# Cross-attention on one core: product 7 of y split once more in batches 3 to 6 and 8, T4 formed by ScalarE and accumulating DMAs in batches 3 to 8

## The chip, the core and the metric

The kernel runs on one core of one Trainium2 chip. Its engines work side by side, each through its own instructions in order: TensorE (PE, with its weight loads shown apart as PEld) multiplies matrices into PSUM, VectorE (DVE) and ScalarE (ACT) work element by element and read PSUM, GpSimd (POOL) reduces over partitions and issues DMAs, SyncE (SP) issues DMAs. Every wait between engines is a semaphore. The metric is the time of one execution in microseconds of the device; all times below are microseconds unless ns stands beside them.

## The reference

Eight batches; x (called x1 in the kernel) and ctx (x2) are 8 x 512 x 1024, FP32.

```python
q = jnp.einsum('bcn,dc->bnd', x1, Wq) + bq
k = jnp.einsum('bcn,dc->bdn', x2, Wk) + bk[:, None]
v = jnp.einsum('bcn,dc->bdn', x2, Wv) + bv[:, None]
attn = jax.nn.softmax(jnp.einsum('bnd,bdm->bnm', q, k), axis=2)
attn_out = jnp.einsum('bcm,bnm->bcn', v, attn)
return attn_out + x1
```

D is 64, C is 512, N is 1024. Since each row of attn sums to one, the kernel multiplies in another order: y = x2 times the transposed attn, then out = Wv y + bv + x1.

## The kernel before

Numbers of batches: the code counts `s.b` from 0 to 7, so batch 3 of the title is `s.b == 2`, and batch 8 is `s.b == 7`.

**Two stages, seven products each.** Stage y (`first(i)` in `period`) multiplies the 512 x 1024 matrix x2 by the 1024 x 1024 matrix of exponentials, stage o (`second(i)`) multiplies Wv by y. Both use Winograd's form of Strassen's scheme: each operand is cut into 2 x 2 blocks, four sums are made of the left blocks (S1 to S4) and four of the right ones (T1 to T4), and seven products take the place of eight. `MULT` (L290) lists for each product its two operands and its PSUM bank: products 1, 6, 5 and 3 add up in bank a, 7 and 4 in bank c (2 opens bank c and leaves block 11 there). Each bank is a pair of tiles, a0 and a1 or c0 and c1, for the two halves j of 128 rows. After products 1, 6 and 5, ScalarE copies the running sum out of bank a into `s.tmp[i]` (tags u1, u6, u5; L323), since the result blocks need each of the partial sums. `RESULT` (L456) says what each block is: 11 = bank c + u1, 22 = bank c after product 7 + u5, 12 = bank a after product 3, 21 = bank c after product 4 + u6. VectorE forms these in `evict_y` and `evict_o`; in stage y, step 1 adds, step 2 multiplies by the reciprocal denominators `rden`.

**A second cut.** Some products of stage y are themselves computed by the same scheme, with blocks of 128 x 256: `multiply_2`, `multiply_3` and `multiply_4`. `inner_left` and `inner_right` make the eight inner sums on VectorE (L344, L355), `inner_product` (L358) multiplies. In `multiply_onto` (used for 3 and 4) the inner products 2, 4 and 3 go straight onto the outer bank (`b0` left, `b1` left, `b0` right); inner product 1, then 6, then 5 add up in a buffer `chain` of the two-buffer tag `sc`, and 7 goes to `third`, the other `sc` buffer. ScalarE copies chain after 1, after 6 and twice after 5 into `d`, and third into `v` (L371); then `complete` adds v to d on VectorE (L431), and what d holds is added to the result. The inner products run in the order 1, 7, 6, 2, 5, 4, 3.

**Softmax.** The scores of the next batch n, two halves h of four tiles i, are multiplied in between (L190), by way of `sc` buffers and, for i = 2, bank c (h = 0) or bank a (h = 1). ScalarE copies them out (`e`, L199 and L197), VectorE folds the maximum over tiles (L210, L214), GpSimd reduces it over partitions (`highest`, L220), VectorE subtracts it (`lower`, L248) and ScalarE exponentiates (L252). Denominators: for h = 0 `start_sum` copies tile 0 on ScalarE and adds the others by accumulating DMAs of POOL (`add_tile`, L521); for h = 1 VectorE adds (L210). `total` reduces over partitions on POOL (L225) and starts a DMA (`few`); `shares` takes the reciprocal (L233) and spreads it by DMAs of POOL.

**Order.** The whole order is written by hand (`manual_schedule`): each engine runs what it is given in the order in which `period` (L671) calls it. In batches 2 to 5 (as `s.b` counts) it reads: first(1); T1, T2 and the sums of h = 1; multiply_2 and its evictions; T4 (`sum_t4`, L270), S4 and T3 on VectorE; first(6); the inner sums of T4 and S4; the scores of h = 0 and the next queries; their maxima; first(5); `lower` and the exponentials; inner sums of product 3's right operand; first(7); inner sums of block 22; multiply_3; blocks 22 and 12 out of PSUM; multiplication by `rden`; the scores of h = 1 and the next keys; T1, T2 of y; multiply_4; block 21; then second(1), 6, 2, 5, 7, 3, 4 with their evictions, and between them the sums and inner sums of the next batch. Batch 7 has no next batch: no scores, queries or keys stand between its products.

**Buffers.** Tags with one buffer tie steps together: eT4 holds T4 and, at the end of a period, the inner sums for the next batch's product 2; eT2 holds T2 and then the inner sums of T4; u5 holds product 5's copy and then product 4's d; i2 is multiply_2's; yT1, yT2, yT4 and y12 hold sums and blocks of y in stage o. x2 and x1 of later batches are loaded through one buffer x (L125), block tiles of x2's transpose by L132, results go out by L517 (x1 added to them by an accumulating DMA of POOL) and L518.

Of the kernel before, what the change touches and what calls it, by code (L numbers as in the profile page):

```python
# [15 lines left out]
def kernel(  # L16
# [8 lines left out]
    bv: bass.AP,  # L25
    out: bass.AP,
):

# [71 lines left out]
    def left_sums(a, *ks):  # L100

        for k in ks:
            x, y, op = {
                "S1": ("21", "22", ALU.add),
                "S2": ("S1", "11", ALU.subtract),
                "S3": ("11", "21", ALU.subtract),
                "S4": ("12", "S2", ALU.subtract),
            }[k]
            nc.vector.tensor_tensor(a["21" if k == "S3" else k], a[x], a[y], op)  # L109
            if k == "S3":  # L110
                a["S3"] = a["21"]
# [145 lines left out]

    def right_sums(t, k):

        x, y = {"T1": ("12", "11"), "T2": ("22", "T1"), "T3": ("22", "12"), "T4": ("21", "T2")}[k]  # L260
        nc.vector.tensor_tensor(t[k], t[x], t[y], ALU.subtract)  # L261

    def open_t(s):
        for n in ("T1", "T2"):
# [3 lines left out]
        s.t["T3"] = s.t["12"]  # L268

    def sum_t4(s):  # L270
        s.t["T4"] = sb.tile([P, MH, H], F32, tag="eT4", name=f"eT4_{s.b}")
        sum_e(s, "T4")

    def sum_e(s, *ks):
        for i in (0, 2):
            part = {n: v[:, i : i + 2, :] for n, v in s.t.items()}
            for k in ks:
                right_sums(part, k)
# [18 lines left out]
        4: ("22", "T4", "c", False),  # L297
    }

    def multiply(s, stage, i, left, right, n_k, last=False):  # L300


        ka, kb, bank, opens = MULT[i]
        for j in range(2):
            if opens:
                s.bank[bank, j] = ps_a.tile(
                    [P, H], F32, tag=f"{bank}{j}", name=f"ps_{stage}{bank}{j}_{s.b}_{i}"
                )
            ps = s.bank[bank, j]
            for n in HALVES if last and j else (slice(0, H),):  # L310
                for k in range(n_k):
                    nc.tensor.matmul(  # L312
                        ps[:, n],
                        left[ka][:, k, ts(j, P)],
                        right[kb][:, k, n],
                        start=opens and k == 0,
                        stop=i in (2, 3, 4) and k == n_k - 1,
                        skip_group_check=True,
                    )
            if i in (1, 6, 5):  # L320
                if j == 0:
                    s.tmp[i] = sb.tile([P, 2, H], F32, tag=f"u{i}", name=f"u{stage}{i}_{s.b}")
                nc.scalar.copy(s.tmp[i][:, j, :], ps)  # L323

    LEFT = (
        ("S1", "21", "22", ALU.add),
        ("S2", "S1", "11", ALU.subtract),
        ("S3", "11", "21", ALU.subtract),
        ("S4", "12", "S2", ALU.subtract),
    )  # L330
    RIGHT = (
        ("T1", "12", "11", ALU.subtract),
        ("T2", "22", "T1", ALU.subtract),
        ("T3", "22", "12", ALU.subtract),
        ("T4", "21", "T2", ALU.subtract),
    )
# [10 lines left out]
    def inner_right(s, i, x, tag):  # L347
# [4 lines left out]
        sums = sb.tile([P, 4, MH // 2, H // 2], F32, tag=tag, name=f"eI{i}_{s.b}")  # L352
        for z, (k, x, y, op) in enumerate(RIGHT):
            v[k] = sums[:, z]
            nc.vector.tensor_tensor(v[k], v[x], v[y], op)  # L355
        s.inner[i, "t"] = v

    def inner_product(s, i, z, ps, opens, *copies):  # L358

        ka, kb, _, _ = MULT[z]  # L360
        for k in range(MH // 2):
            nc.tensor.matmul(  # L362
                ps,
                s.inner[i][ka][:, k, :],
                s.inner[i, "t"][kb][:, k, :],
                start=opens and k == 0,
                stop=z in (2, 3, 4) and k == MH // 2 - 1,
                skip_group_check=True,
            )
        for copy in copies:  # L370
            nc.scalar.copy(copy, ps)  # L371
# [35 lines left out]

        return evict

    def multiply_onto(s, i, d_tag, v_tag):  # L410

        b0, b1 = (s.bank[MULT[i][2], j] for j in range(2))
        chain, third = inner_bank(s, i, 0), inner_bank(s, i, 2)
        d = sb.tile([P, 2, 2, H // 2], F32, tag=d_tag, name=f"d{i}_{s.b}")
        v = sb.tile([P, 2, H], F32, tag=v_tag, name=f"v{i}_{s.b}")[:, 0, left]
        for z, ps, opens, *copies in (
            (1, chain, True, d[:, 0, 0, :]),
            (7, third, True, v),  # L420
            (6, chain, False, d[:, 1, 0, :]),
            (2, b0[:, left], False),
            (5, chain, False, d[:, 0, 1, :], d[:, 1, 1, :]),
            (4, b1[:, left], False),
            (3, b0[:, right], False),
        ):
            inner_product(s, i, z, ps, opens, *copies)

        def complete():
            both = v.unsqueeze(1).to_broadcast([P, 2, H // 2])  # L430
            nc.vector.tensor_tensor(d[:, 1], d[:, 1], both, ALU.add)  # L431

        return d.rearrange("p j a n -> p j (a n)"), complete

    def multiply_4(s):

        d, complete = multiply_onto(s, 4, "u5", "r")
        complete()
        for j in range(2):
            u6 = s.tmp[6][:, j, :]  # L440
            nc.vector.tensor_tensor(u6, u6, d[:, j, :], ALU.add)

    def multiply_3(s):

        d, complete = multiply_onto(s, 3, "u1", "r")

        def evict():
            complete()
            s.y["12"] = y = sb.tile([P, 2, H], F32, tag="y12", name=f"y12_{s.b}")
            for j in (1, 0):  # L450
                nc.vector.tensor_tensor(y[:, j, :], s.bank["a", j], d[:, j, :], ALU.add)

        return evict
# [4 lines left out]
    def evict_y(s, k, steps=(1, 2)):  # L458

        bank, add = RESULT[k]  # L460
        rden = s.rden.get(int(k[1]) - 1)
        if 1 in steps:
            s.y[k] = sb.tile([P, 2, H], F32, tag=f"y{k}", name=f"y{k}_{s.b}")
        y = s.y[k]
        for step in steps:
            for j in range(2):
                ps = s.bank.get((bank, j))
                if add is None and step == 1:
                    nc.vector.tensor_tensor(y[:, j, :], ps, rden, ALU.mult)
                elif step == 1:  # L470
                    nc.vector.tensor_tensor(y[:, j, :], ps, s.tmp[add][:, j, :], ALU.add)
                else:
                    nc.vector.tensor_tensor(y[:, j, :], y[:, j, :], rden, ALU.mult)

# [45 lines left out]
    def add_tile(s, h, i):  # L520
        nc.gpsimd.dma_start(s.mx[h], s.e[h][:, :, i, :], accum_op=ALU.add)  # L521

    def start_sum(s, h):

        e = s.e[h]
        s.mx[h] = f = sb.tile([P, 2, H], F32, tag="fold", name=f"sum_{s.b}_{h}", bufs=2)
        nc.scalar.copy(f, e[:, :, 0, :])
        for i in range(1, MH if s.b > 1 else 2):  # L530
            add_tile(s, h, i)

# [138 lines left out]
    def period(s, n, nn, nnn):  # L671

        def first(i):
            multiply(s, "y", i, s.a, s.t, MH)

        def second(i):
            multiply(s, "o", i, w, s.y, 2, n is None and i == 3)
# [31 lines left out]
        if n:  # L711
            load_a(n, "21", "22")
        first(6)
        if s.b:
            inner_right(s, 4, s.t["T4"], "eT2")
            inner_left(s, 3, s.a["S4"], "aI3")

        def next_queries():
            queries(nn)
# [17 lines left out]
        first(5)  # L737
        if s.b == 0:
            inner_right(s, 3, s.t["22"], "eT1")
            for i in range(MH):  # L740
                lower(n, 0, i)
        elif n:
            for i in range(MH):
                exponentials(n, 0, i)
            start_sum(n, 0)
        if s.b:
            inner_right(s, 3, s.t["22"], "eT1")
        first(7)
        if s.b > 1:
            inner_left(s, 4, s.a["22"], "a12")  # L750
        evict_3 = multiply_3(s)
        if s.b:
            evict_y(s, "22", (1,))
            evict_3()
        else:
            evict_3()
            evict_y(s, "22", (1,))
        for k in ("11", "12", "22"):
            evict_y(s, k, (2,))
        if s.b == 1:  # L760
# [102 lines left out]
```

## Time and profile before

Three runs took 695.27, 695.43 and 696.22; the median is 695.43. One execution was profiled:

| | |
|---|---|
| profiled execution, its time | 694.83 |
| its span, first to last instruction | 693.0 |
| granted TensorE clock | 1.00 throughout |
| VectorE, sum of T2 or T4, 128x1024 (L261 eT<-e,eT) | 32 of them, mean 1489 ns |
| VectorE, inner sums of a right operand, 128x512 (L355) | 683 to 688 ns each |
| VectorE, inner sums of a left operand, 128x256 (L344) | 418 to 497 ns each |
| ScalarE, copy of 128x512 out of PSUM (L323) | 587 ns |
| ScalarE, copy of 128x1024 in SBUF (L529) | 1031 ns |
| ScalarE, copy of an inner product, 128x256 (L371) | 372 to 375 ns |
| POOL, issue of an accumulating DMA (L521) | 1224 ns, landing 5.1 later (median) |
| POOL, all-reduce of a denominator (L225) | mean 4337 ns |
| POOL, all-reduce of a maximum (L220) | mean 1957 ns |

The mean of one instruction is from its start to its end; VectorE and ScalarE overlap the end of one with the start of the next by some 0.1, so that a sequence is read from start to start in the timeline. First(1) of the batches starts at 204.0 (`s.b` = 2), 288.4, 372.7, 457.2, 541.7 and 619.5 (`s.b` = 7).

### The profile page before, as it was taken

The numbers are of one execution on the slowest core, as the hardware profiler recorded it, in microseconds if no ns is written. First come the engines' busy times: TensorE is split into PE (matmuls) and PEld (weight loads), VectorE is DVE, ScalarE is ACT, GpSimd is POOL, SyncE is SP. The second block draws the span as 40 slices with busy tenths as digits, with TensorE's granted clock in tenths as the row PEclk, the third lists the DMA queues.
The fourth block names the chain that finished last, engine by engine and source line by source line (L and its number), as shares of the span: only waits on it lengthen the run. The fifth ranks groups of instructions, "written<-read, shape, count | busy, mean of one in ns | idle before, by whom it ended". The sixth has DMA issues, their size and how long they took to land.

```text
span 693.0 us, 6395 instructions
## 1 busy us (share of the span) xinstructions
PE 685.8 (99%) x2188; PEld 353.4 (51%) x2188; DVE 604.5 (87%) x756; ACT 255.2 (37%) x402; POOL 186.9 (27%) x135
## 2 busy tenths in 40 slices
PE   8999999999999999999999999999999999999997
PEld 5333554535545355454654546454554545545563
DVE  1999999988999878998789987999689998999685
ACT  2733353145242543235432344413444235241120
POOL 0123113512322125222162222522223222423000
PEclk9999999999999999999999999999999999999999
DMA  9676256953567463865639457284742743369103
GB/s 307 254 233 226 58 183 129 260 157 76 183 128 210 149 116 142 166 183 151 107 138 191 157 166 181 67 190 140 183 78 55 172 136 60 77 115 251 31 1 121
DMA packets 42992, 102.72 MB, mean 148 GB/s; under 512 B 4688, under 2 KB 6992, under 8 KB 42960
## 3 DMA queue, kind: packets, MB, share of 16 engines
q1 hardware_dynamic: 25856, 70.13, 29.1%
q0 software_dynamic: 15696, 29.96, 25.7%
q10 hardware_dynamic: 1408, 2.23, 1.0%
q8 instruction: 17, 0.28, 0.2%
q14 instruction: 15, 0.12, 0.0%
HBM read 72.62 MB, written 16.81 MB: 129 GB/s over the span
## 4 chain that ended last, share of the span: by engine, by line
PE 95%; DMA 2%; ACT 1%; DVE 1%; SPq 1%; issue 0%; DVEq 0%
PE ps_ya L312 24%; PE ps_oa L312 16%; PE ps_i L362 14%; PE ps_oc L312 12%; PE ps_yc L312 9%; PE ps_s L190 6%; PE ps_k L148 4%; PE ps_q L148 4%; PE ps_yc L362 3%; PE ps_ya L362 3%; DMA a<-in_x2T_dram 1%; DMA x_head<-in_x_dram 1%; PE ps_sc L190 1%; PE ps_sa L190 1%; DVE aS L109 0%; ACT e L199 0%
## 5 line engine op out<-in xcount | busy, mean ns | idle before, releaser
L312 PE MATMUL ps_ya<-eT,aS 128*128 128x512 f32 x256 | 113.1, 596 | 0.0
L323 ACT COPY uy<-ps_ya 128x512 f32<-128x512 f32 x48 | 28.0, 587 | 163.8 <-PE ps_ya L312 158.0
L225 POOL PARTITION_ALL_REDUCE den<-sum x16 | 69.4, 4337 | 44.0 <-DVE sum L214 39.0
L248 DVE TENSOR_TENSOR e<-e,top 128x1024 f32<-128x1024 f32 x60 | 69.8, 1215 | 10.9 <-POOL top L220 10.9
L312 PEld LDWEIGHTS ps_ya<-eT,aS 128*128 128x128 f32 x256 | 48.0, 190 | 60.8 <-issue 59.7
L220 POOL PARTITION_ALL_REDUCE top<-max x16 | 31.3, 1957 | 162.4 <-DVE few L233 74.9
L252 ACT ACTIVATE e<-e 128x1024 f32<-128x1024 f32 x60 | 61.3, 1054 | 21.6 <-DVE e L248 20.1
L362 PE MATMUL ps_i<-eI,aI 128*128 128x256 f32 x276 | 66.0, 380 | 0.3 <-ACT e L199 0.3
L312 PE MATMUL ps_yc<-e,a 128*128 128x512 f32 x144 | 63.4, 593 | 0.0
L312 PE MATMUL ps_oa<-yT,w_S 128*128 128x512 f32 x128 | 57.6, 593 | 0.0
L312 PE MATMUL ps_oc<-y,w 128*128 128x512 f32 x128 | 57.5, 592 | 0.0
L312 PE MATMUL ps_ya<-e,a 128*128 128x512 f32 x128 | 56.3, 593 | 0.3 <-ACT e L243 0.3
L362 PEld LDWEIGHTS ps_i<-eI,aI 128*128 128x128 f32 x276 | 51.9, 190 | 8.2 <-ACT e L199 0.7
L199 ACT COPY e<-ps_s 128x1024 f32<-128x1024 f32 x46 | 45.7, 1028 | 19.1 <-PE ps_s L190 17.9
L323 ACT COPY uo<-ps_oa 128x512 f32<-128x512 f32 x48 | 27.9, 584 | 64.3 <-PE ps_oa L312 58.1
L190 PE MATMUL ps_s<-q,k 64*128 64x512 f32 x188 | 47.3, 608 | 0.8 <-ACT q L553 0.8
L261 DVE TENSOR_TENSOR eT<-e,eT 128x1024 f32<-128x1024 f32 x32 | 47.0, 1489 | 0.5
L312 PEld LDWEIGHTS ps_yc<-e,a 128*128 128x128 f32 x144 | 27.3, 190 | 34.8 <-issue 33.6
L521 POOL DMA_DIRECT2D sum<-e x21 | 25.7, 1224 | 69.5 <-DMA sum<-e 54.8
L371 ACT COPY d<-ps_i 128x256 f32<-128x256 f32 x64 | 22.3, 375 | 57.9 <-PE ps_i L362 57.9
L517 POOL DMA_DIRECT2D uo<-in_x_dram x21 | 25.0, 1191 | 68.9 <-DVE uo L514 63.1
L312 PEld LDWEIGHTS ps_ya<-e,a 128*128 128x128 f32 x128 | 24.3, 190 | 31.3 <-issue 29.6
(119 smaller groups left out, 1098.7 us busy)
## 6 DMA issues: line engine op xcount, KB each, us to landing
x_in_x_dram<-in_x_dram SPq DMA_DIRECT2D x60, 512.0 KB, 6.0
a<-in_x2T_dram SPq DMA_DIRECT2D x32, 512.0 KB, 7.0
sum<-e POOLq DMA_DIRECT2D x21, 512.0 KB, 5.1
uo<-in_x_dram POOLq DMA_DIRECT2D x21, 512.0 KB, 6.5
out_dram<-uo SPq DMA_DIRECT2D x21, 512.0 KB, 4.1
den<-row POOLq DMA_DIRECT2D x16, 256.0 KB, 3.5
r<-in_x_dram POOLq DMA_DIRECT2D x7, 512.0 KB, 5.9
out_dram<-r SPq DMA_DIRECT2D x7, 512.0 KB, 8.3
```

What stands on the lines that cost most here:

```text
L148: nc.tensor.matmul(ps[r, :], w_sb[:, c, :], s.x[:, c, ts(h, H)], start=(c == 0), stop=(c == CT - 1),)
L190: nc.tensor.matmul(ps[g], s.k[r, ts(i, P)], s.q[r, ts(h, H)], start=True, stop=True)
L199: nc.scalar.copy(e[:, :, i, :], whole)
L220: nc.gpsimd.partition_all_reduce(s.top[h], s.mx[h][:, 0, :], P, ReduceOp.max)
L225: nc.gpsimd.partition_all_reduce(s.den[h], s.mx[h][:, 0, :], P, ReduceOp.add)
L248: nc.vector.tensor_tensor(e, e, top, ALU.subtract)
L252: nc.scalar.activation(e, e, AF.Exp)
L261: nc.vector.tensor_tensor(t[k], t[x], t[y], ALU.subtract)
L312: nc.tensor.matmul(ps[:, n], left[ka][:, k, ts(j, P)], right[kb][:, k, n], start=opens and k == 0, stop=i in (2, 3, 4) and k == n_k - 1, s ...
L323: nc.scalar.copy(s.tmp[i][:, j, :], ps)
L362: nc.tensor.matmul(ps, s.inner[i][ka][:, k, :], s.inner[i, "t"][kb][:, k, :], start=opens and k == 0, stop=z in (2, 3, 4) and k == MH // 2 ...
L521: nc.gpsimd.dma_start(s.mx[h], s.e[h][:, :, i, :], accum_op=ALU.add)
```

## The change

Product 7 of stage y is computed by `multiply_onto` in the batches with `seven` (`s.b` from 2 to 5, and 7). It opens bank c itself, in the inner order 1, 2, 7, 6, 4, 5, 3; its inner sums lie in yT4, yT1 and yT2, its d in i2, its v in y12. `add_7` adds the completed d to u5 and u6, which block 22 and block 21 are formed with. The right half of c1 is not written, so that these blocks take that quarter from u5 or u6 alone. In these batches the exponentials of h = 0 and the DMAs that add them up are called from hooks between the inner products, `lower` comes before first(5), and T4's inner sums come after block 12 has left PSUM. The last batch keeps product 4's d in a buffer of a21.

In batches with `s.b` from 2 on, T4 is formed by two ScalarE copies of block 21 and two accumulating DMAs that add T2. For this T2 and S2 have their signs turned (and T4 and S4 add them), in the outer sums and in the inner ones. In batch 6, T4's inner sums move behind first(7), and those of block 22 ahead of the scores.

```diff
-                "S2": ("S1", "11", ALU.subtract),
+                "S2": ("11", "S1", ALU.subtract),
                 "S3": ("11", "21", ALU.subtract),
-                "S4": ("12", "S2", ALU.subtract),
+                "S4": ("12", "S2", ALU.add),
...
-        x, y = {"T1": ("12", "11"), "T2": ("22", "T1"), "T3": ("22", "12"), "T4": ("21", "T2")}[k]
-        nc.vector.tensor_tensor(t[k], t[x], t[y], ALU.subtract)
+        x, y = {"T1": ("12", "11"), "T2": ("T1", "22"), "T3": ("22", "12"), "T4": ("21", "T2")}[k]
+        nc.vector.tensor_tensor(t[k], t[x], t[y], ALU.add if k == "T4" else ALU.subtract)
...
     def sum_t4(s):
-        s.t["T4"] = sb.tile([P, MH, H], F32, tag="eT4", name=f"eT4_{s.b}")
-        sum_e(s, "T4")
+        s.t["T4"] = t4 = sb.tile([P, MH, H], F32, tag="eT4", name=f"eT4_{s.b}")
+        if s.b < 2:
+            sum_e(s, "T4")
+            return
+        for i in (0, 2):
+            nc.scalar.copy(t4[:, i : i + 2, :], s.t["21"][:, i : i + 2, :])
+        for i in (0, 2):
+            nc.gpsimd.dma_start(t4[:, i : i + 2, :], s.t["T2"][:, i : i + 2, :], accum_op=ALU.add)
...
                 nc.scalar.copy(s.tmp[i][:, j, :], ps)
+                if hook and j == 0:
+                    hook()
...
-    def multiply_onto(s, i, d_tag, v_tag):
-        b0, b1 = (s.bank[MULT[i][2], j] for j in range(2))
+    def multiply_onto(s, i, d_tag, v_tag, hooks={}):
+        bank, opens = MULT[i][2:]
+        if opens:
+            for j in range(2):
+                s.bank[bank, j] = ps_a.tile([P, H], F32, tag=f"{bank}{j}", name=f"ps_y{bank}{j}_{s.b}_{i}")
+        b0, b1 = (s.bank[bank, j] for j in range(2))
         chain, third = inner_bank(s, i, 0), inner_bank(s, i, 2)
...
+        steps = {
+            1: (chain, True, d[:, 0, 0, :]),
+            7: (third, True, v),
+            6: (chain, False, d[:, 1, 0, :]),
+            2: (b0[:, left], opens),
+            5: (chain, False, d[:, 0, 1, :], d[:, 1, 1, :]),
+            4: (b1[:, left], opens),
+            3: (b0[:, right], False),
+        }
+        for z in (1, 2, 7, 6, 4, 5, 3) if opens else (1, 7, 6, 2, 5, 4, 3):
+            inner_product(s, i, z, *steps[z])
+            if z in hooks:
+                hooks[z]()
...
-        d, complete = multiply_onto(s, 4, "u5", "r")
+        d, complete = multiply_onto(s, 4, "u5" if s.b < B - 1 else "a21", "r")
...
+    def multiply_7(s, hooks):
+        d, complete = multiply_onto(s, 7, "i2", "y12", hooks)
+        def add():
+            complete()
+            for k in (5, 6):
+                nc.vector.tensor_tensor(s.tmp[k], s.tmp[k], d, ALU.add)
+        return add
...
+        alone = 7 in s.inner and add in (5, 6)
         for step in steps:
             for j in range(2):
+                if step == 1:
+                    ps, n = s.bank[bank, j], left if alone and j else slice(0, H)
+                    nc.vector.tensor_tensor(y[:, j, n], ps[:, n], s.tmp[add][:, j, n], ALU.add)
+                elif alone and j:
+                    for x, n in ((y, left), (s.tmp[add], right)):
+                        nc.vector.tensor_tensor(y[:, j, n], x[:, j, n], rden[:, n], ALU.mult)
...
+        seven = 2 <= s.b < B - 2 or n is None
...
         first(6)
+        if s.b == 1:
+            inner_right(s, 4, s.t["T4"], "eT2")
         if s.b:
-            inner_right(s, 4, s.t["T4"], "eT2")
             inner_left(s, 3, s.a["S4"], "aI3")
+        if s.b > 1 and not seven:
+            inner_left(s, 4, s.a["22"], "a12")
+        if seven:
+            inner_left(s, 7, s.a["S3"], "yT4")
+            inner_right(s, 7, s.t["T3"], "yT1", "yT2")
+
+        def add_exponential(i):
+            exponential(n, 0, i)
+            add_tile(n, 0, i)
...
+        if seven:
+            hooks = [{}, {}]
+            if n:
+                for i in range(MH):
+                    lower(n, 0, i)
+                hooks = [
+                    {
+                        1: lambda: copy_first(n, 0),
+                        6: lambda: add_exponential(1),
+                        5: lambda: add_exponential(2),
+                    },
+                    {6: lambda: add_exponential(3)},
+                ]
+            first(5, (lambda: exponential(n, 0, 0)) if n else None)
+            inner_right(s, 3, s.t["22"], "eT1")
             inner_left(s, 4, s.a["22"], "a12")
+            add_7 = multiply_7(s, hooks[0])
+            add_7()
+            evict_3 = multiply_3(s, hooks[1])
             evict_y(s, "22", (1,))
             evict_3()
+            inner_right(s, 4, s.t["T4"], "eT2")
         else:
...
+            first(7)
+            if s.b > 1:
+                inner_right(s, 4, s.t["T4"], "eT2")
+            evict_3 = multiply_3(s, {})
```

More of the change, by code (lines that the diff above doesn't have):

```diff
@@ L298, with multiply @@
     }
-    def multiply(s, stage, i, left, right, n_k, last=False):
+    def multiply(s, stage, i, left, right, n_k, last=False, hook=None):
         ka, kb, bank, opens = MULT[i]
@@ L323, in multiply @@
                 nc.scalar.copy(s.tmp[i][:, j, :], ps)
+                if hook and j == 0:
+                    hook()
     LEFT = (
         ("S1", "21", "22", ALU.add),
-        ("S2", "S1", "11", ALU.subtract),
+        ("S2", "11", "S1", ALU.subtract),
         ("S3", "11", "21", ALU.subtract),
-        ("S4", "12", "S2", ALU.subtract),
+        ("S4", "12", "S2", ALU.add),
     )
@@ L332 @@
         ("T1", "12", "11", ALU.subtract),
-        ("T2", "22", "T1", ALU.subtract),
+        ("T2", "T1", "22", ALU.subtract),
         ("T3", "22", "12", ALU.subtract),
-        ("T4", "21", "T2", ALU.subtract),
+        ("T4", "21", "T2", ALU.add),
     )
@@ L345, in inner_left, with inner_right @@
         s.inner[i] = v
-    def inner_right(s, i, x, tag):
+    def inner_right(s, i, x, *tags):
         v = {
@@ L351, in inner_right @@
         }
-        sums = sb.tile([P, 4, MH // 2, H // 2], F32, tag=tag, name=f"eI{i}_{s.b}")
+        shape = [P, 4 // len(tags), MH // 2, H // 2]
+        sums = [sb.tile(shape, F32, tag=t, name=f"eI{i}{t}_{s.b}") for t in tags]
         for z, (k, x, y, op) in enumerate(RIGHT):
-            v[k] = sums[:, z]
+            v[k] = sums[z // shape[1]][:, z % shape[1]]
             nc.vector.tensor_tensor(v[k], v[x], v[y], op)
@@ L408, in multiply_2 @@
         return evict
-    def multiply_onto(s, i, d_tag, v_tag):
-        b0, b1 = (s.bank[MULT[i][2], j] for j in range(2))
+    def multiply_onto(s, i, d_tag, v_tag, hooks={}):
[4 more added lines that the diff above has]
+        b0, b1 = (s.bank[bank, j] for j in range(2))
         chain, third = inner_bank(s, i, 0), inner_bank(s, i, 2)
-        d = sb.tile([P, 2, 2, H // 2], F32, tag=d_tag, name=f"d{i}_{s.b}")
+        d = sb.tile([P, 2, 2, H // 2], F32, tag=d_tag, name=f"d{i}_{s.b}", bufs=1 + (d_tag == "a21"))
         v = sb.tile([P, 2, H], F32, tag=v_tag, name=f"v{i}_{s.b}")[:, 0, left]
[L418 to L427, printed above, removed]
+        steps = {
[11 more added lines that the diff above has]
+                hooks[z]()
         def complete():
@@ L441, in multiply_4, with multiply_3 @@
             nc.vector.tensor_tensor(u6, u6, d[:, j, :], ALU.add)
-    def multiply_3(s):
-        d, complete = multiply_onto(s, 3, "u1", "r")
+    def multiply_7(s, hooks):
[5 more added lines that the diff above has]
+        return add
+    def multiply_3(s, hooks):
+        d, complete = multiply_onto(s, 3, "u1", "r", hooks)
         def evict():
@@ L464, in evict_y @@
         y = s.y[k]
+        alone = 7 in s.inner and add in (5, 6)
         for step in steps:
             for j in range(2):
[L467 to L471, printed above, removed]
+                if step == 1:
[4 more added lines that the diff above has]
+                        nc.vector.tensor_tensor(y[:, j, n], x[:, j, n], rden[:, n], ALU.mult)
                 else:
@@ L521, in add_tile, with copy_first @@
         nc.gpsimd.dma_start(s.mx[h], s.e[h][:, :, i, :], accum_op=ALU.add)
+    def copy_first(s, h):
+        s.mx[h] = sb.tile([P, 2, H], F32, tag="fold", name=f"sum_{s.b}_{h}", bufs=2)
+        nc.scalar.copy(s.mx[h], s.e[h][:, :, 0, :])
     def start_sum(s, h):
-        e = s.e[h]
-        s.mx[h] = f = sb.tile([P, 2, H], F32, tag="fold", name=f"sum_{s.b}_{h}", bufs=2)
-        nc.scalar.copy(f, e[:, :, 0, :])
+        copy_first(s, h)
         for i in range(1, MH if s.b > 1 else 2):
@@ L671, in period, with first @@
     def period(s, n, nn, nnn):
-        def first(i):
-            multiply(s, "y", i, s.a, s.t, MH)
+        seven = 2 <= s.b < B - 2 or n is None
+        def first(i, hook=None):
+            multiply(s, "y", i, s.a, s.t, MH, hook=hook)
         def second(i):
@@ L736, in period @@
         shares(s, 1)
-        first(5)
-        if s.b == 0:
-            inner_right(s, 3, s.t["22"], "eT1")
[L740 to L749, printed above, removed]
+        if seven:
[12 more added lines that the diff above has]
+            first(5, (lambda: exponential(n, 0, 0)) if n else None)
+            inner_right(s, 3, s.t["22"], "eT1")
             inner_left(s, 4, s.a["22"], "a12")
-        evict_3 = multiply_3(s)
-        if s.b:
+            add_7 = multiply_7(s, hooks[0])
+            add_7()
+            evict_3 = multiply_3(s, hooks[1])
             evict_y(s, "22", (1,))
             evict_3()
+            inner_right(s, 4, s.t["T4"], "eT2")
         else:
-            evict_3()
-            evict_y(s, "22", (1,))
+            first(5)
+            if s.b == 0:
+                inner_right(s, 3, s.t["22"], "eT1")
+                for i in range(MH):
+                    lower(n, 0, i)
+            else:
+                for i in range(MH):
+                    exponentials(n, 0, i)
+                start_sum(n, 0)
+                inner_right(s, 3, s.t["22"], "eT1")
+            first(7)
+            if s.b > 1:
+                inner_right(s, 4, s.t["T4"], "eT2")
+            evict_3 = multiply_3(s, {})
+            if s.b:
+                evict_y(s, "22", (1,))
+                evict_3()
+            else:
+                evict_3()
+                evict_y(s, "22", (1,))
         for k in ("11", "12", "22"):
```

## The prediction

> Batches are called 0 to 7 here, as `s.b` counts them: the change's "batches 3 to 6 and the last" are 2, 3, 4, 5 and 7. A record is one row of the trace; an FP32 matmul of the code is two records (8 matmuls of `multiply` show as x16).
>
> **What bounds the kernel now.** I read the busy table, then the chain of waits, then the windows cut at the starts of the batches.
>
> ```profile
> PE 685.8 (99%) x2188; PEld 353.4 (51%) x2188; DVE 604.5 (87%) x756; ACT 255.2 (37%) x402; POOL 186.9 (27%) x135
> PE 95%; DMA 2%; ACT 1%; DVE 1%; SPq 1%; issue 0%; DVEq 0%
> 372.90:457.40 84.50, 84.50 (x269) 43.62 (x269) 73.90 (x94) 31.96 (x50) 25.92 (x17) 1.00 0.59 153
> ```
>
> TensorE is the bound: in batch 4 (third line: length, then busy time of PE, PEld, DVE, ACT, POOL, then granted clock 1.00) it has no gap. A batch is 84.46 us from one first(1) to the next. So a microsecond of records taken off PE is one gained, as long as nobody makes PE wait; VectorE has 84.5 - 73.9 = 10.6 us of idle time per batch to pay from. The rows that the steps rest on (timeline: start, length, engine, line):
>
> ```profile
> 406.79 7.03 PE L312 MATMUL ps_yc<-e,a 128*128 128x512 f32 x16
> 413.66 1.03 PE L362 MATMUL ps_i<-e,aS 128*128 128x256 f32 x4
> 417.98 1.03 PE L362 MATMUL ps_ya<-eI,aS 128*128 128x256 f32 x4
> 419.80 1.99 PE L190 MATMUL ps_s<-q,k 64*128 64x512 f32 x8
> ...
> 418.18 0.65 ACT L371 COPY d<-ps_i 128x256 f32<-128x256 f32 x2 [1.35 <-PE ps_i L362]
> ...
> 388.76 2.34 DVE L261 TENSOR_TENSOR eT<-e,eT 128x1024 f32<-128x1024 f32 x2
> ```
>
> Whole product 7 runs from 406.79 to 413.66, 6.87 us. Product 3 in blocks has seven inner products of four 256-wide records, 0.86 us each from start to start.
>
> **Product 7 in blocks (2, 3, 4, 5, 7).** Removed: 16 records, 6.87. Added: 28 records of 256. Multiply_2 is such a block product without a break: 379.60 to 385.64, 6.04. Gain 0.83 a batch, 4.15 in five. Here a rule speaks against the change: the Trainium skill, "TensorE: Matmul & The Clock Gate", section "Back-to-back issue gap", says that in a stream of weight loads and matmuls the spacing is set by both, and gives 131 ns at width 512 but 81 at 128, so that narrow matmuls lose. Halfway between (106, an estimate) is 0.81 of the wide one; 28 x 0.81 x 0.43 = 9.7 us, 2.9 worse a batch. The trace disagrees: 256-wide records start 0.216 apart, half of 0.429, with a 0.19 us load each. I take the row.
>
> **The new order inside product 7.** It runs 1, 2, 7, 6, 4, 5, 3, so after inner product 5 only one (0.86) is left before product 3 starts in the same `sc` buffer. ACT's two copies after 5 end 0.86 after 5's natural end (417.98 is that end, 418.18 + 0.65 = 418.83 theirs). That is a dead heat, and the release must still reach PE. Batch 6 has that hand-off late:
>
> ```profile
> 589.08 1.06 ACT L199 COPY e<-ps_s 128x1024 f32<-128x1024 f32 x1
> ...
> 590.19 1.35 PE L362 MATMUL ps_i<-eI,aI 128*128 128x256 f32 x5 [0.29 <-ACT e L199]
> ```
>
> The copy's own 1.03 end near 590.11, PE starts 0.08 later, and eight records take 1.83 (the next group starts at 592.02) instead of 1.73, because the weights were not loaded ahead. So: from 0 (the release is instant) to 0.3 (that row's whole gap); I take 0.08 + 0.10 less the 0.01 above, about 0.17 a batch. The exponentials hooked in between don't lengthen it: exp 1 follows the copies of inner product 6 (about 4.0 to 5.0 us after product 7's start, at 0.97 each), and the copies of 5 are due at 5.4. Net gain: 0.83 - 0.17 = **0.66 a batch**.
>
> **VectorE in batches 2 to 5.** Off: T4, 2.34. On: inner_left 7, 4 x 0.37 = 1.47; inner_right 7, 2.52 (the four sums 394.44 to 396.96); in add_7 the completion 0.79 and two 128x1024 adds at 1.2 = 2.4; split evictions about 0. Net +4.8 of the 10.6 idle. By place, from first(1)'s start (372.73 in batch 4):
> - Up to the maxima it is no later: T4 (2.34) and inner_right 4 (2.52) leave, 3.99 come; the folds still wait for ACT's score copies at 24.9. `lower` starts near 31.3 (32.2 before), so exp 0 is ready before ACT gets to it.
> - Product 7 ends at 40.1, add_7 takes 40.1 to 43.2, y22 until 44.2; y12 needs product 3's copies at 45.4. Cover 1.2; past it every microsecond falls on bank a, which the scores fill 0.6 after y12.
> - inner_right 4 comes behind y12 (47.5 to 49.9), product 4 starts at 53.6: hidden by the scores and keys.
> - y21 ends at 65.3 instead of 64.3 while PE is 0.7 earlier; second(2) wants its product at 66.6. Cover 1.2. Then bank c for second(7): see rival B.
>
> **T4 by ScalarE and DMA (2 to 7).** Two copies of 1.03 on ACT, after multiply_2 leaves eT4 (12.9), before u6's copy at 16.5: ACT is idle there. Two more issues on POOL (1.2 each, as for L521) behind the sum's all-reduce and the few-DMA (about 17 to 19.4); the next on POOL is the maximum, at 29.4. Landing 5.1 each by L521's median; the DMA engines stand idle from about 21 to 28 in batch 4, x2's load starts at 27. T4 is wanted at 47.5 (batch 6: about 37). Hidden, cost 0; without cover a late T4 would stop product 4 one for one, but that is 20 us away. On the queue it is moved past, `shares` and `highest` keep their times. Swapped operands in S2, S4, T2, T4 have the same shapes: 0. Batch 6 drops T4 from VectorE and moves inner sums about; its PE rows have no VectorE wait to remove: 0.
>
> **The last batch.** No scores or keys stand between products 3 and 4:
>
> ```profile
> 658.21 0.69 DVE L431 TENSOR_TENSOR d<-d,v 128x512 f32<-128x512 f32 x1 [4.24 <-ACT d L371]
> 659.01 1.29 DVE L451 TENSOR_TENSOR y<-ps_ya,d 128x512 f32<-128x512 f32 x2
> ...
> 659.06 1.03 PE L362 MATMUL ps_i<-eT,a 128*128 128x256 f32 x4
> 660.21 3.69 DVE L473 TENSOR_TENSOR y<-y,den 128x512 f32<-128x512 f32 x6
> ```
>
> Product 3 starts at 653.01; y12 is out 7.20 later (660.21). Now T4's inner sums start there: T1 7.20, T2 7.91, T3 8.52, T4 9.12 to 9.72. Product 4's second inner product is number 7, with T3; PE gets to it at 6.05 + 0.86 = 6.91, and T3 ends at 9.2. With release and unloaded weights PE waits about **2.4** (at least 1.9, if y12 comes out 0.5 sooner; 3.0 if it waits for all four sums). What follows (yT2, y21) is later by the same order but still ahead of PE. Batch 7: 0.83 - 0.17 - 2.4 = a loss of 1.7.
>
> **Sum.** Profiled execution: 694.83, its span 693.0 and 1.8 around it. 694.83 - 4 x 0.66 + 1.7 = 693.9. The median of the runs, 695.43, is 0.6 above that execution: **694.5**. Bounds: hand-off 0 to 0.3 (five times), last wait 1.9 to 3.0: 693.2 to 695.8.
>
> **Rivals.**
> A, faster: the last batch's sums are not waited for and only the hand-off costs: 695.43 - 5 x 0.66 = 692.1 (691.3 without the hand-off). For: PE's longest wait anywhere now is 1.0. Against: the written order puts the sums behind y12, and VectorE's rows leave no room.
> B, slower: VectorE is held by POOL's all-reduce. In batch 5 it costs VectorE 2.05 (first line: 3.26 for a sum that takes 1.21 in batch 4), in batches 2 to 4 POOL yields instead and takes 7.54:
>
> ```profile
> 522.87 3.26 DVE L261 TENSOR_TENSOR yT<-y,yT 128x1024 f32<-128x1024 f32 x1
> ...
> 528.32 1.40 DVE L514 SCALAR_TENSOR_TENSOR uo<-ps_oc,bv_sb,uo 128x512 f32<-128x512 f32 x2
> ...
> 531.36 3.60 PE L312 MATMUL ps_oc<-y,w 128*128 128x512 f32 x8
> ```
>
> There block 11 leaves bank c at 529.7, 1.6 before second(7) wants it (last line). The change puts VectorE 2.1 later against second(1), so each batch with such a hold loses 0.5, and 1.4 if the maximum's all-reduce takes its 0.85 too (2.13 for 1.28 at 597.33 in batch 6). In all four: 2.2 to 5.6, so 696.7 to 700.1, say 698.4. It decides from a hold of about 1.6 on. The Trainium skill, "GPSIMD Engine Reference", Specifications, says that GpSimd's SBUF interfaces are shared with VectorE for instructions with two SBUF inputs. By that alone T4's two DMA issues would take back the 2.4 that they free; but the L521 issue at 412.73 left the sums beside it at 0.42 (T4's removal costs nothing then), so I charge sharing to all-reduces only.
> C: nothing moves, since what PE saves it waits for elsewhere in each batch (695.4).
>
> **Chances.** This measurement tells from no change what differs by over 0.2%, 1.4 us. Forecast 0.50 (0.20 of it below 694.04, 0.30 within); A 0.15; B 0.28; C 0.02; 0.05 for something slower that I don't see. Faster 0.35, within 0.32, slower 0.33. Range: A's 692.0 to B's middle, 698.8; the forecast's own is 693.2 to 695.8.
>
> **What would show it.** First(1) to first(1) 83.8 in batches 2 to 5; 28 records in 6.04 for product 7; a PE wait on ACT d ahead of product 3 of about 0.1 to 0.2; in the last batch one PE wait of some 2.4 on DVE eI in product 4. Wrong if that wait is absent (A), if PE waits on DVE uo ahead of second(7) or on DVE y at the scores (B), or if ACT's copies slip behind the hooked exponentials.

## The result, and the profile after

In 20 runs beside 20 of the kernel before, the changed kernel takes 693.44 in the median (693.09 to 697.42) against 695.47: a ratio of 0.9975, 95% interval 0.9965 to 0.9985. That is 1.1 under the predicted 694.5, inside the forecast's own range, and by the prediction's bound of 0.2% a small gain. 4 of the 20 runs, all of them above 695, show a granted clock of 0.997 or 0.998 where the others show 0.999 or 1.000, and on another chip (run `e9` below) those were the majority.

The profiled execution took 693.62, its span 691.8, the clock 1.00; it is compared with the 694.83 and 693.0 of before. First the busy table and the chain of waits of the changed kernel:

```profile
PE 682.8 (99%) x2248; PEld 364.2 (53%) x2248; DVE 628.9 (91%) x809; ACT 276.1 (40%) x439; POOL 193.5 (28%) x147
PE 93%; DMA 3%; DVE 1%; SPq 1%; ACT 1%; issue 0%; DVEq 0%
```

PE still carries 93% of the chain (95% before); it is busy for 3.0 us less in 60 more records (five times 12: 28 for 16). VectorE gained 24 us and ScalarE 21, and neither has become the bound. Windows of both kernels, cut at first(1) of a batch (length; busy time of PE, PEld, DVE, ACT, POOL; granted clock; DMA). Batch 4 and the last batch up to second(1), after:

```profile
371.45:455.09 83.64, 83.64 (x281) 45.84 (x280) 79.74 (x108) 35.77 (x57) 28.13 (x19) 1.00 0.69 167
616.61:663.90 47.29, 45.01 (x161) 30.32 (x160) 42.53 (x65) 12.29 (x27) 9.01 (x9) 1.00 0.61 144
```

and before:

```profile
372.73:457.19 84.46, 84.46 (x269) 43.59 (x268) 73.89 (x93) 31.96 (x50) 25.92 (x17) 1.00 0.59 153
619.50:665.10 45.60, 45.60 (x149) 28.16 (x148) 38.50 (x56) 8.53 (x20) 7.54 (x7) 1.00 0.52 126
```

The account closes with these. Batches 2 to 5 take 83.64 to 83.67 where they took 84.46, each without a gap on PE: 0.79 to 0.82 less, 3.20 in four. The last batch takes 1.69 more. Batch 6 is as long as it was (77.85 for 77.84); up to first(1) of batch 2 this execution is 0.3 later. -3.20 + 1.69 + 0.3 = -1.2, which is the difference of the spans. The medians differ by more, 2.03: the kernel before was profiled in an execution 0.6 below its median, the changed kernel in one 0.2 above its own, and for these remaining 0.8 there is no trace. In the last batch PE is busy for 45.01 of 47.29: the gap is in the list of PE's waits,

```profile
PE ps_i L374 <- DVE eI4eT L367: 2.3, 1, 2.3
```

(total, times, longest), and in the timeline (start, length, engine, line). PE:

```profile
655.34 1.03 PE L374 MATMUL ps_i<-eT,a 128*128 128x256 f32 x4
658.65 1.97 PE L374 MATMUL ps_i<-eI4eT,aI 128*128 128x256 f32 x8 [2.28 <-DVE eI4eT L367]
```

and VectorE beside it:

```profile
654.49 0.69 DVE L452 TENSOR_TENSOR d<-d,v 128x512 f32<-128x512 f32 x1 [1.16 <-ACT d L383]
655.29 1.29 DVE L483 TENSOR_TENSOR y<-ps_ya,d 128x512 f32<-128x512 f32 x2
...
657.82 0.68 DVE L367 TENSOR_TENSOR eI4eT<-eT 128x512 f32<-128x512 f32 x1
658.42 0.68 DVE L367 TENSOR_TENSOR eI4eT<-eT,eI4eT 128x512 f32<-128x512 f32 x1
```

Block 12 leaves bank a from 655.29 on, T4's inner sums follow, and PE has done inner product 1 and stands from 656.37. It starts at 658.65, 0.15 after the third sum (657.82 + 0.68), while the fourth is still being made: it waited for T3 alone, the operand of inner product 7. From product 4's start to second(1) are 8.56 (655.34 to 663.90); without the wait they are 6.04 (`e2` below). Of these 2.52, product 7 in blocks wins 0.83 back, which leaves the 1.69. The first of VectorE's lines shows more: VectorE had been idle for 1.16 just before, waiting for the copies of product 3.

Product 7 in batch 4, PE and then ScalarE:

```profile
405.51 1.03 PE L374 MATMUL ps_i<-e,a 128*128 128x256 f32 x4
...
410.69 1.03 PE L374 MATMUL ps_yc<-e,aI 128*128 128x256 f32 x4
411.56 1.03 PE L374 MATMUL ps_i<-e,aS 128*128 128x256 f32 x4
```

```profile
410.89 0.65 ACT L383 COPY d<-ps_i 128x256 f32<-128x256 f32 x2 [0.40 <-PE ps_i L374]
```

From 405.51 to 411.56 are 6.05, against 6.87 for the whole product. ScalarE ends its two copies at 411.54, and product 3 starts at 411.56 without a wait.

### The profile page after: what moved, and what is told of

Same layout as the page of the kernel before. It is cut to its first block, busy times and chain, and to the rows that moved or that the text cites. A ratio compares the mean times of both kernels' runs of the same rounds, so it can differ in the third digit from the quotient of the medians.

```text
span 691.8 us, 6647 instructions
## 1 busy us (share of the span) xinstructions
PE 682.8 (99%) x2248; PEld 364.2 (53%) x2248; DVE 628.9 (91%) x809; ACT 276.1 (40%) x439; POOL 193.5 (28%) x147
## 4 chain that ended last, share of the span: by engine, by line
PE 93%; DMA 3%; DVE 1%; SPq 1%; ACT 1%; issue 0%; DVEq 0%
PE ps_ya L321 24%; PE ps_i L374 17%; PE ps_oa L321 16%; PE ps_oc L321 12%; PE ps_s L191 6%; PE ps_yc L374 5%; PE ps_q L149 4%; PE ps_k L149 3%; PE ps_yc L321 3%; PE ps_ya L374 3%; DMA a<-in_x2T_dram 1%; DMA x_in_x_dram<-in_x_dram 1%; DMA x_head<-in_x_dram 1%; PE ps_sc L191 1%; PE ps_sa L191 1%; DVE aS L110 0%
## 5 line engine op out<-in xcount | busy, mean ns | idle before, releaser
L253 ACT ACTIVATE e<-e 128x1024 f32<-128x1024 f32 x60 | 62.9, 1059 | 38.6 <-DVE e L249 37.1
L221 POOL PARTITION_ALL_REDUCE top<-max x16 | 32.8, 2052 | 150.8 <-DVE max L215 78.9
L226 POOL PARTITION_ALL_REDUCE den<-sum x16 | 63.4, 3961 | 40.8 <-DVE sum L215 35.8
L383 ACT COPY d<-ps_i 128x256 f32<-128x256 f32 x84 | 29.3, 374 | 47.7 <-PE ps_i L374 47.2
L321 PEld LDWEIGHTS ps_oa<-yT,w_S 128*128 128x128 f32 x128 | 24.2, 190 | 30.8 <-issue 29.9
L321 PEld LDWEIGHTS ps_oc<-y,w 128*128 128x128 f32 x128 | 24.1, 190 | 31.0 <-issue 28.9
L211 DVE TENSOR_TENSOR max<-max,e 128x1024 f32<-128x1024 f32 x30 | 36.8, 1225 | 3.0
L507 DVE TENSOR_TENSOR y<-y,den 128x512 f32<-128x512 f32 x54 | 33.8, 683 | 0.0
L238 POOL DMA_DIRECT2D den<-row x16 | 8.9, 557 | 79.0 <-DMA row<-few 73.2
```

The lines of the kernel that those rows point to most:

```text
L211: nc.vector.tensor_tensor(f, e[:, :, 0, :] if i == 1 else f, e[:, :, i, :], op)
L221: nc.gpsimd.partition_all_reduce(s.top[h], s.mx[h][:, 0, :], P, ReduceOp.max)
L226: nc.gpsimd.partition_all_reduce(s.den[h], s.mx[h][:, 0, :], P, ReduceOp.add)
L253: nc.scalar.activation(e, e, AF.Exp)
L321: nc.tensor.matmul(ps[:, n], left[ka][:, k, ts(j, P)], right[kb][:, k, n], start=opens and k == 0, stop=i in (2, 3, 4) and k == n_k - 1, s ...
```

## The experiments

Every kernel is the changed one with the edit shown, timed beside the kernel before on the same chip (median 695.49 beside `e1` to `e4`, 695.49 beside `e5` to `e8`, 695.43 beside `e9` to `e11`; three chips); ratios are to that. Expectations and title count batches from 1 (their batch 8 is `s.b` 7), the text from 0. None leaves work out; `e5`, `e6` and `e7` do some of it twice.

**The last batch.** Undo the blocks there alone (here and in `e3` the other branch also gets a guard, not shown, since the last batch has no next batch whose exponentials it could make):

```diff
-        seven = 2 <= s.b < B - 2 or n is None
+        seven = 2 <= s.b < B - 2
```

> Batch 8 multiplies product 7 whole again (batches 3 to 6 stay in blocks). Theory: the last batch alone loses 1.7 us by the blocks, since PE waits 2.3 for product 4's inner sums behind block 12; whole, it has no such wait. So about 691.8 us, 0.9948 of the kernel before, and no PE wait on DVE eI4 in the trace. Rival: the last batch gains its 0.8 like the others and the wait only moves idle time about; then 694.3 us, 0.9983.

692.18, ratio 0.9945 (0.9929 to 0.9962), span 689.8. PE has no wait on VectorE left after the start, and the last batch up to second(1) takes 45.60 again. It did cost what it seemed to.

Keep the blocks there, and make T4's inner sums ahead of product 7's sum in the time that VectorE stands idle:

```diff
+            if n is None:
+                inner_right(s, 4, s.t["T4"], "eT2")
             add_7 = multiply_7(s, hooks[0])
...
-            inner_right(s, 4, s.t["T4"], "eT2")
+            if n:
+                inner_right(s, 4, s.t["T4"], "eT2")
```

> In batch 8 alone, T4's inner sums are made ahead of product 7 instead of behind block 12. Theory: VectorE stands idle for 1.8 and 1.2 us there, so the wait of 2.3 and the 0.1 after it go and nothing takes their place: about 691.0 us, 0.9937. Rival: the 2.5 us of sums push add_7, block 22 and block 12 back, and PE waits for bank c or for y instead: 693 us or more, 0.9965 or more.

690.84, ratio 0.993 (0.9914 to 0.9947), the best of the study. The same stretch of its timeline, VectorE and PE:

```profile
646.96 0.68 DVE L367 TENSOR_TENSOR eI4eT<-eT 128x512 f32<-128x512 f32 x1
...
654.00 0.69 DVE L452 TENSOR_TENSOR d<-d,v 128x512 f32<-128x512 f32 x1 [0.49 <-ACT d L383]
```

```profile
654.85 1.03 PE L374 MATMUL ps_i<-eT,a 128*128 128x256 f32 x4
655.71 1.89 PE L374 MATMUL ps_i<-eI4eT,aI 128*128 128x256 f32 x8
```

T4's sums begin at 646.96, some 8 us before block 12 leaves its bank, and product 4 runs through: 6.04 from its start to second(1) (660.89). What pays is VectorE's idle time behind that point: two waits of 1.77 and 1.16 in the changed kernel are 0 and 0.49 here, 2.44 less for 2.5 of sums.

**Which half of the change earns.** T4 by ScalarE and DMA without the blocks:

```diff
-        seven = 2 <= s.b < B - 2 or n is None
+        seven = False
```

> Product 7 whole in every batch; T4 of batches 3 to 8 stays on ScalarE and DMAs. Theory: PE has no less to do and had no wait on VectorE, so the part is worth nothing by itself: 695.5 us, 0.999 to 1.001. Rival one: relieving VectorE is where the gain comes from: 694 us, 0.998 or less. Rival two: 6 MB more of DMA and POOL issues cost: 696.5 us or more.

695.58, ratio 1.0005 (0.9992 to 1.0017): on its own the new T4 is worth nothing. The other way round, the blocks with T4 on VectorE:

```diff
-        if s.b < 2:
-            sum_e(s, "T4")
-            return
-        for i in (0, 2):
...
+        sum_e(s, "T4")
```

> Product 7 in blocks as in the changed kernel, T4 of all batches back on VectorE. Theory: VectorE's 2.3 us come ahead of the maxima, lower ends 2.3 later, and exp 0, which ScalarE meets inside first(5), holds up the copies of product 7; about 1.0 to 1.5 us of PE waits in each of batches 3 to 6: 697.4 to 699.4 us, say 698.4, 1.004. Rival: VectorE's idle time hides them: 693.4 us, 0.997.

696.33, ratio 1.0005 (0.999 to 1.002): neither the 698.4 of the theory nor the 693.4 of the rival, and against the kernel before no difference clear of noise. Its batches 2 to 5 take 84.04, 84.81, 84.34 and 83.96 in the profiled execution, 2.5 more than the changed kernel's in the four, where 4 to 6 were expected. In batch 4, PE and ScalarE:

```profile
411.77 1.13 PE L368 MATMUL ps_i<-eI7yT,aI 128*128 128x256 f32 x4 [0.35 <-ACT d L377]
```

```profile
409.91 1.06 ACT L253 ACTIVATE e<-e 128x1024 f32<-128x1024 f32 x1 [3.90 <-DVE e L249]
410.88 0.56 ACT L326 COPY uy<-ps_ya 128x512 f32<-128x512 f32 x1
411.34 0.38 ACT L377 COPY d<-ps_i 128x256 f32<-128x256 f32 x1
```

VectorE is later by T4's 2.3, so `lower` is late; exponential 0 waits 3.90 for it (1.79 in the changed kernel), and the copies of u5 and of inner product 1, which stand behind it on ScalarE, come late for inner product 6. The new T4 earns nothing alone, but it keeps the blocks free of these waits.

**VectorE's cover ahead of second(7) (rival B).** Repeat one or two of the maximum's folds (1.2 each on VectorE, same values) in batches 2 to 5; `e5` is shown, `e6` has a 2 for the 1:

```diff
+            for i in range(1 if seven else 0):
+                fold(n, 1, 2 + i, "max", ALU.max)
```

> The changed kernel with one of the maximum's folds of h = 1 done twice in batches 3 to 6 (1.2 us more VectorE work, no other result). Theory: the cover that is left on VectorE is about 1.1 us where block 21 must be out for second(2) and 1.5 us where block 11 must leave bank c for second(7); so 0.1 to 0.3 us a batch, 693.5 to 694.6 us, say 693.9. Rival one: the 5 us that VectorE idles in a batch pay for it: 693.4. Rival two: there is no cover any more: 4 x 1.2, 698.2 us.

> The same with two folds done twice (2.4 us more VectorE work a batch in batches 3 to 6). Theory: 2.4 less the cover of 1.1 makes a PE wait of 1.3 us ahead of second(2), or of 0.9 ahead of second(7), in each: about 698 us (697 to 699). Rival one (idle time pays): 693.4. Rival two (no cover): 703 us.

Both miss. One fold: 696.89, ratio 1.0021 (1.001 to 1.0032); two: 704.16, 1.0119 (1.0104 to 1.0134), nearest to the rival without any cover. With one fold every one of the four batches takes 84.93 in the profiled execution (698.69, 1.8 above the median), 1.26 more than 83.67. VectorE, POOL and PE in batch 4:

```profile
442.25 3.26 DVE L262 TENSOR_TENSOR yT<-y,yT 128x1024 f32<-128x1024 f32 x1
...
447.70 1.40 DVE L548 SCALAR_TENSOR_TENSOR uo<-ps_oc,bv_sb,uo 128x512 f32<-128x512 f32 x2
```

```profile
441.29 4.14 POOL L226 PARTITION_ALL_REDUCE den<-sum  x1 [3.29 <-DVE sum L215]
```

```profile
448.50 3.70 PE L321 MATMUL ps_oc<-y,w 128*128 128x512 f32 x8 [1.02 <-DVE uo L548]
```

The all-reduce holds a sum of T2 for 3.26 instead of 1.21, block 11 leaves bank c late, and second(7) waits 1.02. It starts at 448.50, when the first of the two evictions that begin at 447.70 is done and the second still runs (to 449.10): it waits for one half of the bank. In batch 4 of the changed kernel the same place reads

```profile
437.51 7.54 POOL L226 PARTITION_ALL_REDUCE den<-sum  x1 [3.30 <-DVE sum L215]
```

so there POOL yields, VectorE's sum takes 1.21, and block 11 is out 1.5 before second(7) wants it (443.28 for 444.79). But this is the only one of the four batches. In batches 2, 3 and 5 of the same execution VectorE is held as in `e5`; batch 3, POOL, VectorE and PE:

```profile
353.84 4.13 POOL L226 PARTITION_ALL_REDUCE den<-sum  x1 [3.30 <-DVE sum L215]
354.80 3.26 DVE L262 TENSOR_TENSOR yT<-y,yT 128x1024 f32<-128x1024 f32 x1
...
360.25 1.40 DVE L548 SCALAR_TENSOR_TENSOR uo<-ps_oc,bv_sb,uo 128x512 f32<-128x512 f32 x2
...
361.12 3.63 PE L321 MATMUL ps_oc<-y,w 128*128 128x512 f32 x8
```

Block 11 is wholly out at 361.65, 0.53 after second(7) has started, but its first half is out just in time, and the eight records take 3.63 where 3.60 is usual. So the hold of rival B did come, and it cost 0.03: held batches take 83.67, batch 4 takes 83.64. (In the profiled executions of `e1`, `e2` and `e7` to `e11` too, those of batches 2 to 5 that are held take 83.66 to 83.68, the others 83.63 or 83.64.) The hold had used up the cover, and the fold of `e5` is then paid in full: 1.2, and a little for weights that were not loaded ahead. With two folds second(2) waits too (0.7 in each batch), and three of the four batches take 86.18 or 86.19, one 84.60, that in which POOL yielded.

**The hand-off to product 3.** A third copy of inner product 5 of product 7 on ScalarE (0.28 more) should make PE wait if product 3 needs that buffer:

```diff
-            5: (chain, False, d[:, 0, 1, :], d[:, 1, 1, :]),
+            5: (chain, False, *[d[:, 1, 1, :]] * (i == 7), d[:, 0, 1, :], d[:, 1, 1, :]),
```

> The changed kernel with one of ScalarE's two copies behind inner product 5 of product 7 made twice, in batches 3 to 6 and 8: the buffer of the sc tag comes free 0.28 us later. Theory: as the hand-off was a dead heat, PE now waits 0.28, and 0.08 for the release and 0.10 for weights not loaded ahead come on top: 0.45 x 5, 695.7 us. Rival: a late hand-off costs only what it is late: 0.28 x 5, 694.8 us. If there is slack that the trace does not show: 693.4.

And the inner order of the other block products, which ends 5, 4, 3 and so leaves two inner products after 5 instead of one:

```diff
-        for z in (1, 2, 7, 6, 4, 5, 3) if opens else (1, 7, 6, 2, 5, 4, 3):
+        for z in (1, 7, 6, 2, 5, 4, 3):
```

> The changed kernel with product 7's inner products in the order 1, 7, 6, 2, 5, 4, 3 that products 3 and 4 have; inner product 5 then has two behind it, and the hand-off to product 3 cannot be late. Theory, after the trace of the change (0.02 us between the copies' end and product 3): nothing to gain, 693.4 us, the ratio that of the changed kernel. Rival, the prediction's own term: 0.17 x 5 less, 692.6 us.

694.69, ratio 0.9989 (0.9975 to 1.0002), and 695.17, 0.9989 (0.9977 to 1.0001). The periods are those of the changed kernel in both, 83.63 to 83.67; the medians lie higher because 5 and 7 of the 12 runs show the clock at 0.997 or 0.998, and of the other seven and five all but one lie within 693.1 to 694.4, as the changed kernel's do. With the third copy, ScalarE and then PE:

```profile
410.69 0.93 ACT L383 COPY d<-ps_i 128x256 f32<-128x256 f32 x3 [0.40 <-PE ps_i L374]
```

```profile
411.35 1.03 PE L374 MATMUL ps_i<-e,aS 128*128 128x256 f32 x4
```

Product 3 starts while the third copy still reads. So it does not write into product 7's `chain`: it opens in the other buffer, that of `third`, which was copied out long before.

**The same kernels on a third chip, and one step further.** The changed kernel unaltered, `e2` unaltered, and `e2` with blocks in batch 6 too:

> The changed kernel as it is, beside e10 on the same chip. Theory: the 2.3 us in which TensorE idles in batch 8 sometimes bring its clock down for some 2 to 4 us, so its times fall into two groups, near 693.3 and near 695.3 us. Rival: the two groups come from the start of the kernel (the first matmuls), and e10 shows them as much.

> As e2 (batch 8's inner sums of T4 ahead of product 7). Theory: without the idle time there is no second group from it: nearly all runs within 690.6 to 691.2 us, 2.4 us under e9's lower group. Rival: two groups 2 us apart as in e9.

```diff
-        seven = 2 <= s.b < B - 2 or n is None
+        seven = s.b > 1
```

> e10 with product 7 of batch 7 in blocks too. PE has 0.8 us less to do there. Theory: batch 7 has no queries between the scores and first(5), so lower ends later against PE; exp 0 holds ScalarE's copies up (about 1.3 us of PE wait on ACT d) and block 12 comes late for bank a (0.4): 691.7 us, 0.9 over e10. Rival: the gain holds as in batches 3 to 6: 690.0 us.

The changed kernel: 695.28, ratio 0.9989 (0.9979 to 0.9999), two runs at 693.4 and nine from 694.89 to 696.03. `e2` again: 691.04, 0.9932 (0.9919 to 0.9945). With batch 6: 696.31, 1.001 (0.9999 to 1.002), a loss as expected but far larger (691.7 was the theory). Two waits make most of it, in batch 6 on PE:

```profile
573.32 1.13 PE L374 MATMUL ps_i<-eI7yT,aI 128*128 128x256 f32 x4 [1.68 <-ACT d L383]
...
591.50 2.08 PE L374 MATMUL ps_i<-eI4eT,aI 128*128 128x256 f32 x4 [2.31 <-ACT d L383]
```

The first, foreseen as 1.3, is in product 7, whose copies stand behind the exponentials on ScalarE. The second was not foreseen: it is in product 4, whose d goes into u5, and ScalarE's copy into it waits 3.06 for a multiplication on VectorE that still reads u5 (L505). The four records after it take 2.08 where 1.03 is usual, and the granted clock is 0.50 from 592 to 594 (see the last section). Batch 6 takes 83.12 for 77.85. A product in blocks ties PE to copies, and batch 6 has no slack for them.

## Why the prediction came out as it did

- **PE is the bound, and narrow records cost half of wide ones: right.** 6.05 for product 7, 0.79 to 0.82 less a batch (0.83 foreseen). The row was right against the rule of the back-to-back gap, by which the prediction's estimate made each batch 2.9 longer.
- **The hand-off, 0.17 a batch: wrong.** This is the step that failed: "so after inner product 5 only one (0.86) is left before product 3 starts in the same `sc` buffer". It is not the same buffer, as `e7` shows. The term was 0 instead of 0.85 in five batches. With 0 the sum is 694.5 - 0.85 = 693.65, beside 693.1 to 693.6 in 14 of the first 20 runs. That it then lies so near is partly luck: without its 0.6 for the median the sum gives 693.08 for the profiled execution, which took 693.62 (of the 0.54 between, 0.3 lie before batch 2), while the median came out 0.2 below that execution and not 0.6 above it.
- **The last batch, a wait of 2.4 and a loss of 1.7: right,** 2.28 and 1.69, at product 4's second inner product and for T3 as written. Two small errors cancel in the 1.7: wait and unloaded weights together made 2.52 instead of 2.4, and no hand-off was paid.
- **T4 hidden at cost 0: right** by `e3`. Its DMAs landed later than the 5.1 taken: 8.7 to 10.6 in the last batch, still far ahead of product 4. That it frees VectorE is what the blocks need (`e4`).
- **VectorE's cover: right ahead of second(2), underestimated ahead of second(7).** Product y21 leaves 1.1 before second(2) (436.81 for 437.92; 1.2 foreseen). Ahead of second(7) VectorE comes 2.2 later against PE in a held batch (block 11 wholly out 1.64 before second(7) in batch 5 of before, 0.53 after its start now), as foreseen. But the 0.5 a batch that was to follow was 0.03.
- **Rival A** was refuted for the change as it stands and names what is to be had: with the wait taken away by order the kernel goes to 690.8 (`e2`) and 691.0 (`e10`), below A's 692.1, and near A without the hand-off (691.3).
- **Rival B** was right about the hold, which came in three of the four batches, and wrong about its cost. The step is "There block 11 leaves bank c at 529.7, 1.6 before second(7) wants it": 529.7 is the end of both halves, and second(7) starts with the first one, as `e5` shows, some 0.6 sooner. `e5` and `e6` show B's mechanism once VectorE is later still. (Its middle is 698.4 by its own sum, not the 698.8 that the range names.)
- **Not foreseen:** that the wait also lowers the clock in some runs. It makes the gain 2.0 or next to nothing (below).

What stays open: what lets `e4` lose less than foreseen. Among runs with the lowered clock it lies about 1 above the changed kernel (696.3 for 695.3), in the profiled execution the four periods make 2.5, and two of its four runs without the lowered clock take 693.70 and 694.41, no more than the changed kernel: the waits do not seem to come in every execution, which no trace here shows.

## What to carry to other kernels

When one engine has no gap, records taken off it are gained in full, but ask of each batch whether the work that covers a new order is there: the order that was safe in four batches made PE wait in the last, which has no scores. Before charging a wait for a buffer, show by the rows of before that the two steps do share it. Where a bank is emptied in halves, count the cover to the half that the next product needs first. And an edit that moves work to where the engine waited for was idle earlier (`e2`) was worth more than the whole change.

## What the runs showed of the hardware that was not expected

**A gap of 2.28 us on PE lowers its clock, not always.** In `e8` the profiled execution caught it. PE, and the windows of 2 us around it (PEclk is the number ahead of the last two):

```profile
658.62 3.10 PE L374 MATMUL ps_i<-eI4eT,aI 128*128 128x256 f32 x8 [2.28 <-DVE eI4eT L367]
```

```profile
658.00:660.00 2.00, 1.38 (x5) 1.21 (x6) 2.00 (x4) 0.00 (x0) 0.00 (x0) 0.82 0.00 0
660.00:662.00 2.00, 2.00 (x7) 1.55 (x6) 2.00 (x4) 0.62 (x2) 0.00 (x0) 0.50 0.00 0
662.00:664.00 2.00, 2.00 (x9) 1.73 (x8) 1.97 (x5) 0.12 (x1) 0.00 (x0) 0.82 0.00 0
```

About 3.4 us go at 0.50 (a mean of 0.82 is 0.7 of 2 us at half clock: 0.7 + 2.0 + 0.7), which loses 1.7, and product 4 takes 10.25 from its start to second(1) (655.31 to 665.56) instead of 8.56. Of the seven profiled executions with this gap of 2.28, `e6` and `e8` show the fall. The runs' mean clock tells how often: of the changed kernel's 31 runs 11 show 0.997 or 0.998, all from 694.89 on, and 18 of the other 20 lie at 694.4 or below. In `e11`, whose longest gap is 2.31, it is 10 of 11; behind its gap of 1.68 the clock stays at 1.00 in the trace. Of the kernels without a wait of that length (`e1`, `e2`, `e3`, `e10`) none of 29 runs does, nor any of the 73 of the kernel before beside them. The Trainium skill, "TensorE: Matmul & The Clock Gate", section "Why this matters for your kernels", warns of gaps above about 3 us; here 2.28 was enough in a third of the runs of the changed kernel. So the wait costs 2.5, and 1.7 again where the clock falls: together the 4.2 by which `e10` lies below the changed kernel on the same chip (691.04 for 695.28).

**POOL's all-reduce and VectorE take turns at yielding.** The same instruction takes 4.14 with VectorE held for 2.05, or 7.54 with VectorE untouched. Which of the two comes differs between executions of one kernel: the changed kernel has VectorE held in batches 2, 3 and 5 in one profiled execution, in 2, 3 and 4 in the other (`e9`). The all-reduce starts 0.96 before the sum in both kinds (353.84 and 354.80, 437.51 and 438.47). What sets it is open.

**The start of PE varies.** In the profiled execution of `e3` the first queries take

```profile
6.34 5.71 PE L586 MATMUL ps_q<-x_head,wqk_sb 128*64 128x512 f32 x16 [0.66 <-DMA x_head<-in_x_dram]
```

where the changed kernel's take 3.65, and first(1) of batch 0 comes at 27.2 instead of 25.0; in the profiled execution of `e9`, one of the two runs of the changed kernel above 694.4 without a lowered clock (694.92), it comes at 26.6. What makes it late is open. Differences of 2 us between two profiled executions are therefore read by stage, never from the spans alone.
